# Attention and binary convolutions on one core: the weighted sums laid out as four column tiles of 32 channels over all 128 rows of keys

## The chip, the core and the metric

One NeuronCore of a Trainium2 chip runs the whole kernel. The metric is device time in microseconds (us), the median of the runs. TensorE makes the matrix products, ScalarE the exponentials and some copies, VectorE elementwise work and sums, GpSimd (POOL) and SyncE (SP) issue transfers. Matrix products go to PSUM, eight banks of 512 fp32 columns on each of 128 partitions.

## The reference

The input x has 8 images of 64 channels and 64 x 64 pixels, fp32. Two layers follow each other.

The first is attention among the N = 4096 pixels of one image, with C = 64 channels:

```
q, k, v = wq x + bq, wk x + bk, wv x + bv        # 1x1, per pixel
q, k    = q - mean(q), k - mean(k)               # over pixels
sim     = softmax(q^T k / sqrt(C))               # N x N per image
out     = sim v + (one vector per image from a second softmax)
x       = x + out
```

The second takes the signs of x, applies binarized convolutions of 1x1, 3x3 and 5x5, normalizes and adds the three, and returns the sum times a gate per channel, plus x.

What matters here is the product `sim v`: for each query pixel n the sum over all 4096 key pixels m of exp(score[n, m]) times v[:, m], divided by the sum of the exponentials.

## The kernel before, in words

**Tiling.** Two images form a pair; their 2 x 64 channels fill the 128 partitions, and there are four pairs. Of a pair, 512 query pixels are a block (QB = 512): eight blocks per pair, 32 in all. The keys go in tiles of 128 (NK = 32 steps per block). The very last block is cut into two parts (`PARTS`): 384 queries in 32 steps, and 128 queries in 8 steps of four key tiles each.

**One step.** `scores` (L573) makes four products for key tile j, one for each half h of its 128 keys and each image b: 64 channels are contracted, 64 keys are the stationary columns and 512 queries stream. They lie in the four 64x64 quarters of TensorE's array, and their results fill a PSUM tile of two banks, keys on partitions, one bank per image. ScalarE takes the exponential of both banks at once (L595) into e, 128 keys x 2 images x 512 queries. `weighted` (L598) contracts over the keys: for each image b and key half h it multiplies the values v (64 keys by 64 channels) with e. It too lies in the four 64x64 quarters. The two halves h of the keys[...] each has a bank of its own, acc0 and acc1, which holds the partial sum over its half of all keys. `summed` (L615) adds the e tiles up for the softmax denominator on VectorE, except for four tiles per block that transfers add up in DRAM.

**The end of a block.** `weighted_out` (L627) copies the two banks to SBUF, o0 by ScalarE (L632) and o1 by VectorE (L633); later `added` (L713) adds the two on VectorE (L717) into x2; `finish` (L719) multiplies by the reciprocals and adds the second softmax's vector and x. Then come the signs for the convolutions.

**The order** is written out by hand; nothing reorders it. The loop in `attend` (L1371) issues `scores` of step j, then `weighted` and `summed` of step j-1, and then what `plan` has put down for step j with `put(step, function)`. At step 0 of a block the last weighted group of the block before is issued, its `weighted_out`, and `mix_rows` (L1125): the queries of the next block and the convolutions of the block three back, as products in 64x64 quarters. `mix_rows` uses acc0, acc1, the score banks and two further banks (m); the convolution products that it leaves in acc0 and acc1 are copied out by `hold`, on ScalarE (L939) and VectorE (L937), and after that the next block's weighted sums begin in them. `added` stands at step 13, `finish` at 15. Of the result tiles x2 there are ten buffers, since they are kept until `store` writes the pair's output in the third and fourth block of the next pair. The tiles o0 and o1 share their buffers with the row differences of the convolutions (`rows5`, `rows3`).

TensorE leaves the 64x64 quarters in a few places only: a 128x128 product once per pair (`unary_end`, L461), one 64x128 product (L223), the column sums of the last block (`sums_wide`, L696, 128 rows by 64 columns), and the beginning and the end of the program.

A slow path at the end of the program (from L1484) is entered only where a softmax without its maximum subtracted would have left the range of fp32; it uses the same functions and is not run on these inputs.

Of the kernel before, what the change touches and what calls it, by code (L numbers as in the profile page):

```python
# [18 lines left out]
F32 = mybir.dt.float32  # L19
# [3 lines left out]
ALU = mybir.AluOpType  # L23
# [3 lines left out]
P = 128  # L27
# [4 lines left out]
QB = 512  # L32
NQ = N // QB
NK = N // P
# [13 lines left out]
def conv_seq_kernel(ctx, tc, x, wqv, wk, wv, w1, w3, w5, wtap, gw, out):  # L48
    nc = tc.nc
# [3 lines left out]
    img = [slice(0, C), slice(C, P)]  # L53
# [3 lines left out]
    bp = ctx.enter_context(tc.tile_pool(name="blocks", bufs=10))  # L57
    ep = ctx.enter_context(tc.tile_pool(name="ep", bufs=5))
    fp = ctx.enter_context(tc.tile_pool(name="fp", bufs=1))
# [3 lines left out]
    ps_a = ctx.enter_context(tc.tile_pool(name="ps_a", bufs=1, space=PSUM))  # L63
# [215 lines left out]
    class Pair:  # L279
# [3 lines left out]
        def __init__(self, name, xt):  # L283
            self.name, self.x = name, xt
            self.xs = sm.tile([P, 8], F32, tag="xs", name=f"xs_{name}")
            self.q, self.x2, self.s, self.y1, self.acc, self.o = {}, {}, {}, {}, {}, {}
            self.sides = []
            self.es, self.r, self.joint, self.sc, self.gap, self.t = {}, {}, None, None, None, None

# [308 lines left out]
        def weighted(self, qb, j, e, part=(slice(0, QB), 1)):  # L598
            cols, n = part
            w = cols.stop - cols.start  # L600
            if j == 0:
                self.acc[qb] = acc_banks(f"acc_{self.name}_{qb}_{cols.start}")
            for t in range(n * j, n * j + n):
                at = (t - n * j) * w
                for b in range(2):
                    for h in range(2):
                        nc.tensor.matmul(  # L607
                            self.acc[qb][h][img[b], 0:w],
                            self.v[img[h], t, img[b]],
                            e[img[h], b, at : at + w],  # L610
                            start=(t == 0),
                            stop=(t == NK - 1),
                        )

        def summed(self, qb, j, e, dram=False, begin=nc.vector):  # L615

# [10 lines left out]
        def weighted_out(self, qb, cols=slice(0, QB)):  # L627

            acc, w = self.acc.pop(qb), cols.stop - cols.start
            if cols.start == 0:  # L630
                self.o[qb] = [self.tile(fp, f"o{h}", qb) for h in range(2)]
            nc.scalar.copy(self.o[qb][0][:, cols], acc[0][:, 0:w])  # L632
            nc.vector.tensor_copy(self.o[qb][1][:, cols], acc[1][:, 0:w])  # L633

# [68 lines left out]
        def reciprocals_wide(self, qb, cols):  # L705
            if cols.start == 0:
                self.r[qb] = self.tile(fp, "r", qb)
            for a in range(cols.start, cols.stop, P):
                c = slice(a, min(a + P, cols.stop))
                sums, at = self.sums_p  # L710
                nc.vector.reciprocal(self.r[qb][:, c], sums[:, c.start - at : c.stop - at])

        def added(self, qb, cols=slice(0, QB)):  # L713
            if cols.start == 0:
                self.x2[qb] = self.tile(bp, "x2", qb)
            o = self.o[qb]
            nc.vector.tensor_tensor(self.x2[qb][:, cols], o[0][:, cols], o[1][:, cols], ALU.add)  # L717

        def finish(self, qb, cols=slice(0, QB)):  # L719
            x2 = self.x2[qb][:, cols]  # L720
# [486 lines left out]
    def acc_banks(name):  # L1207
        return [ps_a.tile([P, QB], F32, tag=f"acc{h}", name=f"{name}_{h}") for h in range(2)]

    def misc_banks(name):  # L1210
        return [m_tile(f"{name}_{h}") for h in range(2)]

# [4 lines left out]
    def attend(pairs, early):  # L1217
# [9 lines left out]
        def plan(g):  # L1227


            at = {}  # L1230

            def put(i, f, *a):
                at.setdefault(i, []).append((f, a))

            pr, qb = divmod(g, NQ)
# [34 lines left out]
            if g >= 1:  # L1270
                put(5, p.fold_first, b)
                put(6, p.fold, b)
                put(7, p.fold_last, b)
                put(8, p.spread, b)
                put(9, p.check_block, b, 0)
                put(11, p.check_block, b, 1)
                at0 = 13 if g < n_blocks - 1 else 11
                put(at0, p.added, b)
                put(at0 + 2, p.finish, b)
                put(at0 + (3 if g < n_blocks - 1 else 4), p.signs_wide, b, 2)  # L1280
                put(at0 + (5 if g < n_blocks - 1 else 6), p.signs_wide, b, 1)
                put(at0 + 7, p.signs, b)
# [63 lines left out]
        def plan_last():  # L1346

            at, (first, _) = {}, PARTS
            for i, steps in plan(n_blocks - 1).items():
                at[i * QB // first[0].stop] = steps  # L1350

            def put(i, f, *a):
                at.setdefault(i, []).append((f, a))

            p, b = pairs[-1], NQ - 1
            cols = first[0]
            r1 = cols.stop // HH
            put(NK - 5, lambda: mix(None, rows(n_blocks - 3), one_bank, score_banks))
            put(NK - 2, lambda: mix(None, (p, p.joint_rows(0, 6)), one_bank, score_banks))
            put(NK, p.weighted_out, b, cols)  # L1360
            put(NK + 1, p.added, b, cols)
            put(NK + 1, p.sums_wide, b, first)
            put(NK + 1, p.reciprocals_wide, b, cols)
            put(NK + 2, p.finish, b, cols)
            put(NK + 3, lambda: p.check(p.r[b][:, cols], n_blocks - 1))
            put(NK + 4, p.signs_wide, b, 2, 0, r1)
            put(NK + 5, p.signs_wide, b, 1, 0, r1)
            put(NK + 6, p.signs, b, 0, r1)
            return at
# [28 lines left out]
        r0, r1 = cols.start // HH, ROWS  # L1398
        p.weighted_out(b, cols)
        p.sums_wide(b, part)  # L1400
        p.added(b, cols)
        p.reciprocals_wide(b, cols)
        p.check(p.r[b][:, cols], n_pairs * (NQ + 1), (0,))
        p.finish(b, cols)
# [1 line left out]
            p.signs_wide(b, n, r0, r1, None)  # L1406
            p.copy_signs(b, n, r0, r1, (nc.vector.tensor_copy, nc.gpsimd.tensor_copy))
        p.signs(b, r0, r1, nc.gpsimd.tensor_copy)

        def acc_bank(h):  # L1410
            return lambda name: [ps_a.tile([P, QB], F32, tag=f"acc{h}", name=name)]

        def count(side):
            p.check(p.r[b][:, cols], n_pairs * (NQ + 1), (side,))
# [69 lines left out]
    with tc.If(n_good < P):  # L1484
        neg = fp.tile([P, QB], F32, tag="t5", name="neg")
        nc.vector.memset(neg, 0.0)
        with tc.For_i(0, n_pairs * P, P) as row:
            rows = bass.ds(row, P)
            p = Pair("g", load_x("g", rows))
            for c in range(4):  # L1490
                p.mean_part(c, quarters[c])
            p.mean_sum()
            p.mean_scores()
            p.mean_scores_out()
            p.minus_mean_scores()
            p.value_weights()
            p.shifted_unary()
            for g in range(NQ):
                p.values(g, unary=False)
            for qb in range(NQ):  # L1500
                mix((p, qb), None)
                for h in range(QB // P):
                    part = sm.tile([P, 2, NQ], F32, tag="part", name=f"part_{qb}_{h}")
                    for kb_ in range(NQ):
                        ps = ps_s.tile([P, 2, QB], F32, tag="s", name=f"px_{qb}_{h}_{kb_}")
                        for b in range(2):
                            nc.tensor.matmul(
                                ps[:, b, :],
                                p.q[qb][img[b], bass.ts(h, P)],
                                p.x[img[b], bass.ts(kb_, QB)],  # L1510
                                start=True,
                                stop=True,
                            )
                        nc.vector.tensor_reduce(part[:, :, kb_], ps, AX.X, ALU.max)
                    nm = sm.tile([P, 2], F32, tag="nmx", name=f"nmx_{qb}_{h}")
                    nc.vector.tensor_reduce(nm, part, AX.X, ALU.max, negate=True)
                    pn = m_tile(f"pn_{qb}_{h}")
                    for b in range(2):
                        nc.tensor.matmul(
                            pn[C * b : C * b + 1, 0:P], nm[:, b : b + 1], ident, start=True, stop=True  # L1520
                        )
                        nc.vector.tensor_copy(
                            neg[C * b : C * b + 1, bass.ts(h, P)], pn[C * b : C * b + 1, 0:P]
                        )
                for j in range(NK):
                    e = p.scores(qb, j, neg)
                    p.weighted(qb, j, e)
                    p.summed(qb, j, e)
                p.weighted_out(qb)
                p.sums_wide(qb)  # L1530
                p.reciprocals_wide(qb, slice(0, QB))
                p.added(qb)
                p.finish(qb)
            p.copy_tile()
            for qb in range(NQ):
                for n in (1, 2):
                    p.signs_wide(qb, n)
            for qb in range(NQ):
                p.signs(qb)
                mix(None, (p, p.rows(qb)), acc_banks, score_banks)  # L1540
            p.gate_mean()
            p.gate()
            for qb in range(NQ):
                p.store(qb, rows)
# [57 lines left out]
```

## Time and profile before

| | |
|---|---|
| median of the runs before | 1893.41 us (2 runs, 1893.37 to 1893.46) |
| the profiled execution's span, first to last instruction | 1889.9 us |
| the profiled execution's own time | not given apart; the median lies 3.5 us above the span |
| TensorE busy | 1875.6 us (99%) |
| VectorE busy | 1602.8 us (85%) |
| ScalarE busy | 1269.5 us (67%) |
| GpSimd busy | 131.2 us (7%) |
| granted TensorE clock, mean | 0.999 |

The profile lists instructions in groups: line of the code, engine, operation, output and inputs by name, tile (rows*columns of the array) and shape, count; then the busy time of the group, the mean duration of one in ns, and how long the engine stood idle before them, with what ended that. PE is TensorE; PEld are its weight loads, which have records of their own. A fp32 matmul has two records, as it goes through the array in two passes. Ends of matmuls are modelled, starts are recorded. The chain of waits goes back from the last instruction, at each step to what released it. In the timeline, neighbours of one kind are merged: start, length from the first start to the last end, what, and how many records.

### The profile page before, as it was taken

To read this page: it belongs to the slowest core of one execution; us is meant where nothing else is said; L and a number is where in the kernel's file an instruction comes from. 1 tells how busy PE (TensorE), PEld (TensorE's weight loads), DVE (VectorE), ACT (ScalarE), POOL (GpSimd) and SP (SyncE) were. 2 spreads that over 40 slices of the span, in tenths; PEclk is the share of its full clock that TensorE was granted. 3 is DMA by queue.
4 is the path that set the end of the run, shared out by engine and by line. 5 is a ranking of instruction groups with operands and counts; after the bars stand their busy time and mean duration, and the time that the engine had idled before them with its cause. 6 is when DMAs were issued, how large, how long until landed. Compare 5 with 4: busy or idle time off the path is not lost.

```text
span 1889.9 us, 51407 instructions
## 1 busy us (share of the span) xinstructions
PE 1875.6 (99%) x22016; PEld 800.7 (42%) x22016; DVE 1602.8 (85%) x2526; ACT 1269.5 (67%) x1630; POOL 131.2 (7%) x176
## 2 busy tenths in 40 slices
PE   9999999999999999999999999999999999999997
PEld 4345344443344434443434444434433344444345
DVE  7888888889888888888888888888888888888886
ACT  6666776666666676666666667666666666666664
POOL 0000000000000000000000000000000000000001
PEclk9999999999999999999999999999999999999999
DMA  4334333333333433333333444243333333333311
GB/s 125 65 65 103 78 67 71 67 58 72 68 70 89 117 82 81 65 73 66 58 72 68 97 111 89 58 83 66 72 67 58 71 78 90 86 71 65 82 36 53
DMA packets 73461, 142.50 MB, mean 75 GB/s; under 512 B 10444, under 2 KB 41480, under 8 KB 73096
## 3 DMA queue, kind: packets, MB, share of 16 engines
q0 software_dynamic: 22320, 81.27, 23.3%
q1 hardware_dynamic: 50328, 56.73, 10.3%
q8 instruction: 174, 2.85, 0.6%
q10 hardware_dynamic: 576, 1.13, 0.2%
q14 instruction: 63, 0.52, 0.1%
HBM read 39.27 MB, written 89.78 MB: 68 GB/s over the span
## 4 chain that ended last, share of the span: by engine, by line
PE 98%; DVE 1%; ACT 0%; DMA 0%; issue 0%; ACTq 0%; DVEq 0%
PE ps L582 46%; PE acc L607 46%; PE z L906 2%; PE pv L414 1%; PE z L996 1%; PE pq L563 1%; DMA es<-e 0%; PE z_5e L906 0%; ACT e L595 0%; PE warm L157 0%; DVE es L625 0%; DVE sb L1069 0%; PE pq L535 0%; PE su L696 0%; DVE es_j L1028 0%
## 5 line engine op out<-in xcount | busy, mean ns | idle before, releaser
L595 ACT ACTIVATE e<-ps 128x1024 f32<-128x1024 f32 (+1 forms) x1030 | 1048.4, 1018 | 568.2 <-PE ps L582 553.0
L625 DVE TENSOR_TENSOR es<-es,e 128x1024 f32<-128x1024 f32 (+1 forms) x842 | 1019.7, 1211 | 192.5 <-ACT e L595 178.2
L582 PE MATMUL ps<-q,x 64*64 64x512 f32 (+2 forms) x8448 | 1090.3, 577 | 1.5 <-DVE q L347 0.8
L607 PE MATMUL acc<-e,v 64*64 64x512 f32 (+2 forms) x8432 | 1085.8, 576 | 1.3 <-ACT e L595 1.3
L607 PEld LDWEIGHTS acc<-e,v 64*64 64x64 f32 x8432 | 335.0, 131 | 545.8 <-ACT e L595 314.8
L582 PEld LDWEIGHTS ps<-q,x 64*64 64x64 f32 x8448 | 359.5, 133 | 483.3 <-issue 262.3
L646 POOL DMA_DIRECT2D es<-e x93 | 80.1, 861 | 903.8 <-ACT e L595 598.7
L976 DVE SCALAR_TENSOR_TENSOR sb<-pt,sb 128x256 f32<-128x256 f32 x174 | 65.8, 418 | 0.0
L906 PEld LDWEIGHTS <-wc 64*64 64x64 bf16 x3364 | 58.8, 106 | 1.7 <-issue 0.8
L646 POOL DMA_DIRECT2D es<-es x31 | 26.6, 857 | 438.6 <-DVE es L625 438.6
L623 DVE TENSOR_TENSOR es<-e,e 128x1024 f32<-128x1024 f32 (+1 forms) x31 | 37.7, 1216 | 17.2 <-ACT e L595 17.2
L906 PE MATMUL z<-ec,wc 64*64 64x128 bf16 x1392 | 51.5, 217 | 0.0
L906 PE MATMUL z<-t,wc 64*64 64x128 bf16 x1392 | 51.1, 216 | 0.1
L754 ACT ACTIVATE s<-x,wqv_s 128x512 bf16<-128x512 f32 (+2 forms) x66 | 46.2, 702 | 0.2 <-DVE x L722 0.2
L939 ACT ACTIVATE pt<-z,frac 128x256 f32<-128x256 f32 (+1 forms) x58 | 30.6, 578 | 16.8 <-PE z L906 16.8
L644 POOL DMA_DIRECT2D es<-e x31 | 17.5, 563 | 334.5 <-ACT e L595 323.3
L633 DVE COPY o<-acc 128x512 f32<-128x512 f32 (+2 forms) x33 | 22.3, 675 | 9.4 <-PE acc L607 9.3
L950 DVE TENSOR_TENSOR pt<-pt 128x384 f32<-128x384 f32 x58 | 29.6, 552 | 0.0
L414 PEld LDWEIGHTS pv<-wx,x 64*64 64x64 f32 x992 | 21.5, 134 | 16.1 <-issue 8.6
L661 DVE TENSOR_TENSOR e_parts<-e_parts 128x512 f32<-128x512 f32 x31 | 21.3, 686 | 6.1 <-DMA e_parts<-es 6.0
L722 DVE SCALAR_TENSOR_TENSOR x<-x,ou,x 128x512 f32<-128x512 f32 (+2 forms) x33 | 24.3, 736 | 1.2
L422 ACT COPY v<-pv 128x512 f32<-128x512 f32 x31 | 18.2, 587 | 8.4 <-PE pv L414 8.4
(201 smaller groups left out, 893.9 us busy)
## 6 DMA issues: line engine op xcount, KB each, us to landing
es<-e POOLq DMA_DIRECT2D x124, 512.0 KB, 5.1
es<-es POOLq DMA_DIRECT2D x31, 512.0 KB, 5.3
e_parts<-es SPq DMA_DIRECT2D x124, 128.0 KB, 3.0
r<-rc SPq DMA_DIRECT2D x62, 128.0 KB, 2.8
out<-sb SPq DMA_DIRECT2D x27, 256.0 KB, 2.9
x<-in_x SPq DMA_DIRECT2D x24, 256.0 KB, 4.3
ec<-t SPq DMA_DIRECT2D x29, 99.0 KB, 4.5
xc<-in_x SPq DMA_DIRECT2D x30, 72.0 KB
```

Of the source, the lines that this page charges most:

```text
L414: nc.tensor.matmul(pv[img[h], b, i * w : (i + 1) * w], self.x[img[b], bass.ds((4 * g + i) * P + h * H, H)], self.wx[img[b], 0:w], start=Tr ...
L582: nc.tensor.matmul(ps[img[h], b, i * w : (i + 1) * w], self.x[img[b], bass.ds((n * j + i) * P + h * H, H)], self.q[qb][img[b], cols], star ...
L595: nc.scalar.activation(e, ps[:, :, 0 : n * w], AF.Exp, scale=1.0 / 8.0)
L607: nc.tensor.matmul(self.acc[qb][h][img[b], 0:w], self.v[img[h], t, img[b]], e[img[h], b, at : at + w], start=(t == 0), stop=(t == NK - 1),)
L623: begin.tensor_tensor(self.es[qb], self.first, e, ALU.add)
L625: nc.vector.tensor_tensor(self.es[qb], self.es[qb], e, ALU.add)
L646: nc.gpsimd.dma_start(out=out, in_=e, accum_op=ALU.add)
L754: nc.scalar.activation(sy[n][0][:, rows, pad : pad + HH], self.x2[qb][:, r0 * HH : r1 * HH].rearrange("p (h w) -> p h w", w=HH), AF.Sign, ...
L906: nc.tensor.matmul(z[img[b], :].rearrange("p (q w) -> p q w", w=HH), wc[k][img[h], n, c * C : c * C + C], src[:, first : first + step + 1 ...
L939: nc.scalar.activation(out, z, AF.Identity, scale=frac[:, by : by + 1])
L950: nc.vector.tensor_tensor(self.pairs[:, :, :, r, :], t[:, 0:3, 0], t[:, 0:3, 1], op)
L976: nc.vector.scalar_tensor_tensor(out, x, by, out, ALU.mult, ALU.add, **gap)
```

## The change

`weighted` no longer cuts the array into 64x64 quarters. Each key tile is contracted over all its 128 keys at once, and the 128 output channels of the two images are cut into four column tiles of 32: g = 0, 1 for the first image and 2, 3 for the second. There are still four products per key tile, each with 512 streaming columns. The two key halves no longer need two partial sums, so one bank, acc0, holds the result; `weighted_out` copies it by ScalarE straight into x2, and the copy by VectorE and `added` are gone. x2 is therefore taken at step 0 of the following block instead of step 13. `acc_bank`, which stood inside `attend`, moves out unchanged. `mix_rows` still uses acc0 and acc1. `scores` and all else stay.

```diff
@@ weighted
             if j == 0:
-                self.acc[qb] = acc_banks(f"acc_{self.name}_{qb}_{cols.start}")
+                self.acc[qb] = acc_bank(0)(f"acc_{self.name}_{qb}_{cols.start}")[0]
             for t in range(n * j, n * j + n):
                 at = (t - n * j) * w
-                for b in range(2):
-                    for h in range(2):
-                        nc.tensor.matmul(
-                            self.acc[qb][h][img[b], 0:w],
-                            self.v[img[h], t, img[b]],
-                            e[img[h], b, at : at + w],
-                            start=(t == 0),
-                            stop=(t == NK - 1),
-                        )
+                for g in range(4):
+                    nc.tensor.matmul(
+                        self.acc[qb][32 * g : 32 * g + 32, 0:w],
+                        self.v[:, t, 32 * g : 32 * g + 32],
+                        e[:, g // 2, at : at + w],
+                        start=(t == 0),
+                        stop=(t == NK - 1),
+                    )
@@ weighted_out
             if cols.start == 0:
-                self.o[qb] = [self.tile(fp, f"o{h}", qb) for h in range(2)]
-            nc.scalar.copy(self.o[qb][0][:, cols], acc[0][:, 0:w])
-            nc.vector.tensor_copy(self.o[qb][1][:, cols], acc[1][:, 0:w])
+                self.x2[qb] = self.tile(bp, "x2", qb)
+            nc.scalar.copy(self.x2[qb][:, cols], acc[:, 0:w])
...
-        def added(self, qb, cols=slice(0, QB)):
-            if cols.start == 0:
-                self.x2[qb] = self.tile(bp, "x2", qb)
-            o = self.o[qb]
-            nc.vector.tensor_tensor(self.x2[qb][:, cols], o[0][:, cols], o[1][:, cols], ALU.add)
...
+    def acc_bank(h):
+        return lambda name: [ps_a.tile([P, QB], F32, tag=f"acc{h}", name=name)]
...
@@ plan, plan_last, the end of attend and the slow path: the calls of added
-                put(at0, p.added, b)
...
-            put(NK + 1, p.added, b, cols)
...
-        p.added(b, cols)
...
-                p.added(qb)
```

More of the change, by code (lines that the diff above doesn't have):

```diff
@@ L285, in __init__ @@
             self.xs = sm.tile([P, 8], F32, tag="xs", name=f"xs_{name}")
-            self.q, self.x2, self.s, self.y1, self.acc, self.o = {}, {}, {}, {}, {}, {}
+            self.q, self.x2, self.s, self.y1, self.acc = {}, {}, {}, {}, {}
             self.sides = []
@@ L1408, in attend @@
         p.signs(b, r0, r1, nc.gpsimd.tensor_copy)
-        def acc_bank(h):
-            return lambda name: [ps_a.tile([P, QB], F32, tag=f"acc{h}", name=name)]
         def count(side):
```

## The prediction

> **What bounds the kernel now.** I read the page's first part, then the chain that ended last, then the costliest groups.
>
> ```profile
> PE 1875.6 (99%) x22016; PEld 800.7 (42%) x22016; DVE 1602.8 (85%) x2526; ACT 1269.5 (67%) x1630; POOL 131.2 (7%) x176
> ...
> PE 98%; DVE 1%; ACT 0%; DMA 0%; issue 0%; ACTq 0%; DVEq 0%
> ...
> L582 PE MATMUL ps<-q,x 64*64 64x512 f32 (+2 forms) x8448 | 1090.3, 577 | 1.5 <-DVE q L347 0.8
> L607 PE MATMUL acc<-e,v 64*64 64x512 f32 (+2 forms) x8432 | 1085.8, 576 | 1.3 <-ACT e L595 1.3
> ```
>
> TensorE is the bound: busy 99%, 98% of the chain, and its two big groups, the scores (L582) and the weighted sums (L607, the line that changes), waited 1.5 and 1.3 us in all. VectorE and ScalarE follow: the list of waits has ScalarE's exponentials waiting for the scores for 553.0 us. So whatever leaves VectorE or ScalarE is worth almost nothing, and whatever a step adds on TensorE is added to the time. A busy TensorE could still hide slack, so I looked at the pitch in the timeline of TensorE, in the middle of the run (start, length of the merged piece, what):
>
> ```profile
> 900.93 1.06 PE L607 MATMUL acc<-e,v 64*64 64x512 f32 x8
> 901.79 1.06 PE L582 MATMUL ps<-q,x 64*64 64x512 f32 x8
> 902.64 1.06 PE L607 MATMUL acc<-e,v 64*64 64x512 f32 x8
> ```
>
> Each group of four fp32 matmuls (eight records: every fp32 matmul is two passes) starts 0.86 us after the one before; from 900.93 to 906.08 there are six, so 0.858 each. The four 64x64 tiles run at once, so a group is two passes of 512 columns, 0.429 us each, 0.838 ns per column. The 1.06 us is longer than the pitch: groups overlap at their ends. There is no slack in the pitch to win.
>
> Now the places where TensorE changes the layout of its tiles. First a 128*128 product (L461) between two 64*64 groups; then a 128*64 product (L696), the only kind with two column tiles over all 128 rows:
>
> ```profile
> 1404.88 1.06 PE L607 MATMUL acc<-e,v 64*64 64x512 f32 x8
> 1405.87 0.49 PE L461 MATMUL po<-vu,ones 128*128 128x130 f32 x2
> 1406.29 1.09 PE L582 MATMUL ps<-q,x 64*64 64x512 f32 x8
> 1407.20 0.61 PE L607 MATMUL acc<-e,v 64*64 64x512 f32 x4
> ```
> ```profile
> 1855.82 0.72 PE L607 MATMUL acc<-e,v 64*64 64x128 f32 x20
> 1856.48 0.87 PE L696 MATMUL su<-es,ones 128*64 128x384 f32 x4
> 1857.27 0.56 PE L582 MATMUL ps<-q,x 64*64 64x128 f32 x12
> ```
>
> The group that a switch ends lasts 1405.87-1404.88 = 0.99 us instead of 0.86: **0.13 us at the exit**. The same exits at 479.38 and 81.39 us last 1.00 and 0.97. The group that begins after a switch lasts 1407.20-1406.29 = 0.91: **0.05 us at the entry**. L461 itself takes 0.42 against 2 x 130 x 0.838 = 0.22 of streaming, 0.20 more; less an exit of 0.10 that is an entry of 0.10, twice that of the 64-column groups: the exposed part is the first weight load, by columns. L696 shows the same: 0.79 against 2 x 384 x 0.838 = 0.64, so 0.15 more (0.05 and 0.10), and its four records fit in two passes, so two column tiles over all 128 rows did run at once.
>
> **What the Trainium skill says.** "TensorEngine Tiling (Array Packing)", Tiling Modes: changing the tiling mode, not only the tile, drains the engine. The trace agrees, 0.10 to 0.14 us at each exit. "TensorE: Matmul & The Clock Gate", LDWEIGHTS: a load takes its columns divided by 1.2, in ns, whatever the rows; for 64 columns 53 ns, the 0.05 us seen. The same page, Part 3: column tiles of 32 overlap (three of them gave 2.38x); the trace shows only two of 64. "Perfetto Trace Analysis", Tensor Engine Instruction: the end of a matmul in the profile is an estimate; so I use differences of starts only.
>
> **The change, part by part.**
>
> 1. *The products.* Before: four of 64 rows and 64 columns of weights; after: four of 128 rows and 32. Same count, same 512 moving columns, four at once: 0.858 us of streaming either way, gain nil. The trace doesn't show four column tiles over all rows. Bounds: 0 (as the two in L696) to a halved rate, +0.858 us per group. I take 0, for L696's reason.
>
> 2. *The layout switches.* The loop issues the scores of step j, then the weighted sums of step j-1, in turn. Scores stay 64*64, so each weighted group now has a switch before and one after. Groups: 31 blocks of 32 steps, the last one's 32 of 384 columns and 8 of 128 (four tiles of keys each): 992 + 32 + 8 = 1032. (Check: 992 x 8 + 32 x 8 + 8 x 32 = 8448 records, the 8432 and 16 that the trace has.) Each step pays: exit of the scores 0.11, entry of the weighted group by 32 columns 0.025 (half of 0.05, an estimate from the 64- and 128-column entries), its exit 0.11, entry of the scores 0.05. Sum **0.295 us**, and 1032 x 0.295 = **304 us**. For the exit I take 0.11, the 81.39 case, where all the groups before it ran at the regular pitch; in the two others the mix ahead had spread the tiles' starts. Bounds per step: 0.23 (exits 0.09, what is left when the 0.02 by which the first and the last of four tiles start apart (7 ns from one to the next in the records of the group at 1406.29) is hidden, no entry for the weights of 32 columns) to 0.405 (exits 0.14, both entries 0.05, and 0.025 for a second pass's load that is not hidden): 237 to 418 us.
>
> 3. *Second copy and addition gone* (L633: 22.3 us in 33 records; L717: 31 x 0.686 + two short ones, about 22 us). Both are on VectorE, which TensorE doesn't wait for; priced at nothing. The last pair, at 1869.6 to 1870.3, is beside the convolutions that TensorE runs without a gap from 1870.71 to 1875.9: also nothing, at most 0.3 us.
>
> 4. *ScalarE's copy stays* (579 ns, L632), now into the result. Its new wait is for a buffer of x2, taken 13 steps sooner; behind it on ScalarE stand the exponentials. There are ten buffers; in the closest case the earlier user is read last by a store at step 15 of the third block of a pair, and the buffer is wanted again at step 0 of the fourth, 17 steps later: nothing. If that cover were gone it would stall ScalarE, which has 620 us idle.
>
> 5. *One bank instead of two.* After the mix of a block, the first weighted group waits for the bank's last reader, the copy of convolution products by ScalarE (17.7 us of weight-load wait in 29 blocks before), now of one bank, not both. The load was let go about 0.07 us ahead of its matmuls' turn (1404.81 and 1404.88); after the change that turn comes later by the exit of the scores. Nothing; without that cover 29 x 0.1 = 3 us.
>
> 6. *Other engines.* The step grows from 1.717 to 2.01 us; the exponential (1.018 us) and the sum on VectorE (1.211 us) fit with more room. They just wait longer.
>
> Sum against the profiled execution: span 1889.9 + 304 = 2193.9; the median of the runs, 1893.41, is 3.5 us above that span, which I keep: **2197 us**, 16% slower. Own range 1893.4 + 237 to 1893.4 + 418: 2130 to 2311.
>
> **The rivals.**
>
> *A: four column tiles over all rows do not stream at full rate.* Each row of the array would feed four different column tiles with fp32, where the scores feed two; nothing in the trace runs so. If they go two by two, each weighted group has 0.858 us more: 1032 x 0.858 = 885, time 2197 + 885 = 3082. Against it: L696's two tiles at full rate, and the skill's three. Chance 0.11.
>
> *B, the other side: the switch is hidden.* Place: the 2064 borders between L582 and L607. Mechanism: the layouts share column bounds and the weights of the next one are loaded behind the running group, so the border costs what it does now. Price 0, time 1893, no change. It decides if a border costs under 1893.4 x 0.02 / 2064 = 18 ns. Against it: the smallest that any of the switches above shows is 100 to 150 ns with its entry, and those between 64*64 and 128*64 are no cheaper than those to 128*128. Chance 0.05.
>
> *C: the tiles don't overlap at all,* so the change doesn't do what it says: three more streams of 0.858 us per group, 1032 x 2.574 = 2656, time about 4850. Against it: L696. Chance 0.03.
>
> **How the numbers follow.** My forecast has 0.81; A 0.11, B 0.05, C 0.03. The range 2130 to 2310 is the forecast's own; the others leave out 0.19. Slower by over 2% (about what a measurement of this kernel can tell from no change): forecast, A and C, 0.95. Within 2%: B but for 0.01, so 0.04; faster 0.01.
>
> **What would show it.** In the timeline after: scores and weighted groups alternate at about 1.02 and 1.00 us instead of 0.86, each with eight records; weight loads of a group start only when the group before has ended, instead of inside it; the idle time of TensorE appears as short gaps or longer first passes. VectorE's busy time falls by about 44 us and its share to about 71%, with no effect on the end. Wrong if the weighted group's pitch is 1.8 us or more (A or C), if the pitch stays 0.86 (B), or if ScalarE's copy becomes what TensorE waits for at the start of each block.

## The result and the profile after

The changed kernel takes **2190.82 us** (2 runs, 2190.74 to 2190.90) against 1893.41 us before: ratio 1.157, 95% interval 1.1537 to 1.1604. It is 16% slower. Its profiled execution spans 2189.0 us, 299.1 us more than before.

The page of the kernel after, its first part, its chain and the two big groups:

```profile
PE 2176.3 (99%) x22016; PEld 486.1 (22%) x22016; DVE 1584.7 (72%) x2460; ACT 1274.9 (58%) x1630; POOL 131.1 (6%) x176
...
PE 99%; DVE 0%; DMA 0%; ACT 0%; SPq 0%; issue 0%; DVEq 0%
...
L582 PE MATMUL ps<-q,x 64*64 64x512 f32 (+2 forms) x8448 | 1115.2, 600 | 1.1 <-DVE q L347 0.8
L606 PE MATMUL acc<-e,v 128*32 128x512 f32 (+2 forms) x8432 | 1090.9, 591 | 0.1
```

TensorE is busy 99% as before, 301 us longer, with the same number of instructions and the same granted clock, 0.999. These lines alone would hide the cause: the busy time of the two groups, 1090.3 and 1085.8 us before, has grown by 24.9 and 5.1 us only. It was that large before because neighbouring groups overlapped in it, and now they hardly do. The mean durations say nearly nothing either (577 to 600 and 576 to 591 ns). What tells it is the pitch, the time from the start of one group to the start of the next. The timeline of TensorE after, in the middle of the run:

```profile
1045.24 1.07 PE L606 MATMUL acc<-e,v 128*32 128x512 f32 x8
1046.23 1.09 PE L582 MATMUL ps<-q,x 64*64 64x512 f32 x8
1047.26 1.07 PE L606 MATMUL acc<-e,v 128*32 128x512 f32 x8
1048.25 1.09 PE L582 MATMUL ps<-q,x 64*64 64x512 f32 x8
```

A weighted group lasts 0.99 us until the next group starts, a score group 1.02 to 1.03, where both had 0.86. The lengths of the pieces (1.07 and 1.09) are about those of before (1.06): a piece ends in a modelled tail of some 0.07 us into the next group, where it was 0.2.

The place of the 128*128 product, the model for the estimate, looks after the change like this:

```profile
1628.33 1.07 PE L606 MATMUL acc<-e,v 128*32 128x512 f32 x8
1629.33 0.49 PE L461 MATMUL po<-vu,ones 128*128 128x130 f32 x2
1629.75 1.09 PE L582 MATMUL ps<-q,x 64*64 64x512 f32 x8
1630.77 1.06 PE L606 MATMUL acc<-e,v 128*32 128x512 f32 x8
```

That place is now no exception: the weighted group ahead of it lasts 1.00 as everywhere, L461 still 0.42, and the scores behind it 1.02, since they too are left by a switch.

The weight loads show a part of the reason. First the timeline of the loads before, then that after:

```profile
902.33 0.15 PEld L607 LDWEIGHTS acc<-e,v 64*64 64x64 f32 x4 [0.37 <-ACT e L595]
902.65 0.17 PEld L607 LDWEIGHTS acc<-e,v 64*64 64x64 f32 x4 [0.16 <-issue]
```
```profile
1046.23 0.21 PEld L582 LDWEIGHTS ps<-q,x 64*64 64x64 f32 x8 [0.84 <-PE ps L582]
1047.25 0.16 PEld L606 LDWEIGHTS acc<-e,v 128*32 128x32 f32 x8 [0.81 <-ACT e L595]
```

Before, the weighted group that began at 902.64 had its first four loads at 902.33, inside the scores. After, all eight loads start with the group, at 1047.25, and none stands ahead of it. The reason given for the wait (ScalarE's e) is only the semaphore that came last; ScalarE was done early (its exponential ran from 1045.38 for 1.02 us), and in the list of waits it now waits longer for TensorE itself:

```profile
ACT e L595 <- PE ps L582: 844.2, 1007, 2.9
```

That was 553.0 us before.

The unmerged starts, those of the single passes, of the step at 1046.23 take the 0.299 us apart. The last of the scores' second passes starts at 1046.735 and the first weighted pass at 1047.255: 0.520, of which 0.429 is streaming. In the other 0.09 nothing new starts; this is called the drain here. The other border has it too (1047.729 to 1048.250). First and second pass of one tile start 0.481 apart in the scores and 0.454 in the weighted group, instead of 0.429: 0.052 for a first load of 64 columns and 0.025 for one of 32. And the four tiles of a group start 7 ns apart, 0.020 from first to last. In the kernel before, each tile of a group follows its own predecessor after 0.429, so this costs nothing; now the next group starts only behind the last tile. Sum: 2 x 0.091 + 0.052 + 0.025 + 2 x 0.020 = 0.299.

### The profile page after: what moved, and what is told of

Read it like the earlier page. It is cut to its first block, busy times and chain, and to the rows that moved or that the text cites. A ratio compares the mean times of both kernels' runs of the same rounds, so it can differ in the third digit from the quotient of the medians.

```text
span 2189.0 us, 51341 instructions
## 1 busy us (share of the span) xinstructions
PE 2176.3 (99%) x22016; PEld 486.1 (22%) x22016; DVE 1584.7 (72%) x2460; ACT 1274.9 (58%) x1630; POOL 131.1 (6%) x176
## 4 chain that ended last, share of the span: by engine, by line
PE 99%; DVE 0%; DMA 0%; ACT 0%; SPq 0%; issue 0%; DVEq 0%
PE ps L582 47%; PE acc L606 47%; PE z L898 2%; PE pv L414 1%; PE pq L563 1%; PE z L988 1%; DMA x<-in_x 0%; PE z_5e L898 0%; DVE sb L1061 0%; PE su L694 0%; PE po L461 0%; DVE sb L1020 0%; DVE es_j L1061 0%; DVE es L624 0%; PE pq L535 0%
## 5 line engine op out<-in xcount | busy, mean ns | idle before, releaser
L595 ACT ACTIVATE e<-ps 128x1024 f32<-128x1024 f32 (+1 forms) x1030 | 1047.5, 1017 | 848.7 <-PE ps L582 844.2
L582 PE MATMUL ps<-q,x 64*64 64x512 f32 (+2 forms) x8448 | 1115.2, 600 | 1.1 <-DVE q L347 0.8
L606 PE MATMUL acc<-e,v 128*32 128x512 f32 (+2 forms) x8432 | 1090.9, 591 | 0.1
L582 PEld LDWEIGHTS ps<-q,x 64*64 64x64 f32 x8448 | 225.7, 131 | 794.4 <-PE ps L582 740.1
L606 PEld LDWEIGHTS acc<-e,v 128*32 128x32 f32 x8432 | 167.5, 108 | 823.6 <-ACT e L595 582.5
L570 DVE TENSOR_SCALAR q<-pq,mx 128x224 f32<-128x224 f32 x30 | 13.5, 451 | 37.9 <-PE pq L563 37.9
L422 ACT COPY v<-pv 128x512 f32<-128x512 f32 x31 | 18.1, 585 | 17.7 <-PE pv L414 17.7
L929 DVE TENSOR_SCALAR pt<-z,frac 128x256 f32<-128x256 f32 x29 | 14.0, 484 | 18.5 <-PE z L898 18.5
```

The costliest lines, as they stand in the source:

```text
L582: nc.tensor.matmul(ps[img[h], b, i * w : (i + 1) * w], self.x[img[b], bass.ds((n * j + i) * P + h * H, H)], self.q[qb][img[b], cols], star ...
L595: nc.scalar.activation(e, ps[:, :, 0 : n * w], AF.Exp, scale=1.0 / 8.0)
L606: nc.tensor.matmul(self.acc[qb][32 * g : 32 * g + 32, 0:w], self.v[:, t, 32 * g : 32 * g + 32], e[:, g // 2, at : at + w], start=(t == 0), ...
```

## The experiments

The theory: each step pays for leaving and entering a layout twice, and nothing else of the change matters. The rivals: the 128*32 products themselves are slow; the single bank or the direct copy makes TensorE wait; VectorE's lost work is worth something.

### The layout alone

```diff
 # from the kernel before; both copies and added stay
-                for b in range(2):
-                    for h in range(2):
...
+                for g in range(4):
+                    nc.tensor.matmul(
+                        self.acc[qb][t % 2][32 * g : 32 * g + 32, 0:w],
+                        self.v[:, t, 32 * g : 32 * g + 32],
+                        e[:, g // 2, at : at + w],
+                        start=(t < 2),
+                        stop=(t >= NK - 2),
+                    )
```

> The new layout alone: the weighted sums on four 128*32 column tiles, but even key tiles go to acc0 and odd ones to acc1, both banks are copied out by ScalarE and VectorE, and added stays. My theory (two layout switches per step, 0.299 us as the trace after shows it) expects the time after, 2191 us within 5, since VectorE's work and the second bank are worth nothing. The rival that the single bank or the copy straight into x2 makes TensorE wait at the start of a block expects it to be clearly below 2191, by 31 times what such a wait costs. If the copy and the addition that were removed had been worth something, it is above 2191.

Measured: 2191.01 us (4 runs, 2190.59 to 2191.12), ratio 1.1578 (1.1559 to 1.1598). The first line of its page:

```profile
PE 2176.3 (99%) x22016; PEld 486.2 (22%) x22016; DVE 1623.8 (74%) x2526; ACT 1272.7 (58%) x1630; POOL 131.1 (6%) x176
```

VectorE works 39.1 us more than in the changed kernel and TensorE is busy for the same 2176.3 us. So the layout makes the whole difference; the bank, the copy and the addition together make none that is seen.

### Half as many switches, and the order's control

```diff
...
-                new = (p, (qb, j, e), part)
-                if pending is not None:
-                    pending[0].weighted(*pending[1], pending[2])
...
-                for f, a in at.pop(i, ()):
-                    f(*a)
-                pending = new
+                waiting.append((p, (qb, j, e), part))
+                if i % 2 == 0:
+                    continue
+                due = waiting[:-2]
+                for d in due:
+                    d[0].weighted(*d[1], d[2])
+                for d in due:
+                    begin = nc.gpsimd if d[2] == PARTS[1] else nc.vector
+                    d[0].summed(*d[1], g < n_blocks - 1, begin)
+                waiting = waiting[-2:]
+                for f, a in [*at.pop(i - 1, ()), *at.pop(i, ())]:
+                    f(*a)
...
```

Made once to the changed kernel:

> The changed kernel with the loop issuing two score groups and then two weighted groups, so that 516 pairs of switches are left of 1032. My theory expects half of the loss: 1893 + 516 x 0.299 = 2047 us less a few, 2035 to 2050, with the second group of each two starting 0.86 us after the first. The rival that the loss sits in the 128*32 products themselves (slower streaming of four column tiles over all rows) expects the time to stay at 2191, and the rival that waits on ScalarE grow with this order expects more.

and once to the kernel before:

> The control for the order: the kernel before, with the same loop of two score groups and two weighted groups, all in 64*64 tiles. Every theory of the layout expects 1893 us within 10. If it is well below or above, the order itself is worth something, and the paired 128*32 kernel is to be compared with this one.

Measured: 2064.90 us (2064.88 to 2065.48), ratio 1.0913 (1.0894 to 1.0931), for the first, and 1927.24 us (1926.64 to 1927.72), ratio 1.0184 (1.0167 to 1.0201), for the control. Both miss what was expected: the order is not free. The timeline of the control, and then that of the 128*32 kernel:

```profile
1002.11 1.90 PE L582 MATMUL ps<-q,x 64*64 64x512 f32 x16
1003.82 1.90 PE L607 MATMUL acc<-e,v 64*64 64x512 f32 x16
1005.54 1.90 PE L582 MATMUL ps<-q,x 64*64 64x512 f32 x16
```
```profile
1000.68 1.92 PE L606 MATMUL acc<-e,v 128*32 128x512 f32 x16
1002.54 1.95 PE L582 MATMUL ps<-q,x 64*64 64x512 f32 x16
1004.41 1.92 PE L606 MATMUL acc<-e,v 128*32 128x512 f32 x16
```

In the middle of a block the control runs at the pitch of before, 1.71 to 1.72 for two groups, so its 35 us are lost elsewhere. The starts in its trace show where. The two score groups behind the mix of a block take 2.47 us instead of 1.72, some 16 us in all; of the 20.2 us for which its scores stood idle (1.5 before), 12.2 lie there, until the copy of convolution products on VectorE (L944) is done. And once in nearly every block, in 29 of them, the scores behind a weighted pair start 0.2 to 1.7 us late and then take 0.1 us more: 14 us. In 27 of these places ScalarE's exponential had waited for VectorE, which cost 0.7 us in all before:

```profile
ACT e L595 <- DVE rec L671: 82.4, 27, 4.3
```

The new loop does two steps' other work in one place, which is likely why; no run takes that apart.

Two 128*32 groups need 1.86 and two score groups with them 1.87 to 1.88, together 0.30 more than the control. That is one pair of switches for two steps, and a second 128*32 group behind a first costs just its streaming: 1.86 is 0.86 and one 1.00. Against its control the kernel loses 137.7 us, 0.267 for each of 516 pairs, where the pitch says 0.30, 154 us. Of the 16 us between, 14 are the late scores: the trace of the 128*32 kernel has the long groups behind the mix too (2.58 instead of 1.88), but no late ones. Halving the switches has taken 42% of the loss away from the changed kernel in time, and half of it from the pitch. Slow 128*32 products would have kept it all.

### The price of two switches alone

```diff
 # from the kernel before, at the head of weighted, ahead of its products
+            if j > 0:
+                nc.tensor.matmul(
+                    self.acc[qb][0][0:32, 0:1], wu[:, 0:32], e[:, 0, 0:1], start=False, stop=False
+                )
```

> The price of two switches alone: the kernel before, its products all in 64*64 tiles, with one added product per step from the second of a block on: 128 rows, 32 columns of zero weights and one moving column, added into the first 32 partitions of acc0 ahead of the weighted group (999 of them). My theory expects each to cost what the weighted groups pay now, 0.299 us, and up to 0.1 more for its own two short passes: 1893 + 999 x 0.30 to 0.40 = 2190 to 2290 us. The rival that the loss sits in the weighted products themselves, not in the switches, expects at most 999 x 0.1, so below 1993.

The control has the same line with 64 rows and 64 columns, `acc[qb][0][img[0], 0:1], wu[img[0], img[0]], e[img[0], 0, 0:1]`:

> The control for the added product: the kernel before, with the same added product of one moving column per step, but on 64 rows and 64 columns of zero weights, so that the layout never changes. My theory expects only the issue of two short passes, no drain: 0 to 0.08 us each, 1893 to 1975 us. The rival that any product added between the groups breaks the overlap, whatever its layout, expects as much as with the 128*32 one, 2190 us or more.

Measured: 2197.33 us (2196.88 to 2198.47), ratio 1.1613 (1.1594 to 1.1632), for the 128*32 one: 305.2 us over the 1892.13 us of before beside it, 0.306 for each of 999. The control took 2002.86 us (2002.15 to 2004.90), ratio 1.0584 (1.0566 to 1.0602): 0.110 each, more than the 0 to 0.08 expected and far less than the rival's. The timeline of TensorE with the 128*32 product:

```profile
1003.18 0.22 PE L604 MATMUL acc<-e,wu 128*32 128x1 f32 x2
1003.34 1.09 PE L611 MATMUL acc<-e,v 64*64 64x512 f32 x8
1004.25 1.04 PE L582 MATMUL ps<-q,x 64*64 64x512 f32 x8
1005.22 0.22 PE L604 MATMUL acc<-e,wu 128*32 128x1 f32 x2
```

The scores (1004.25 to 1005.22) last 0.97, which is 0.11 of drain and exposed starts; the one-column product 0.15 to 0.16, with its own two short passes and a drain; the weighted group, of 64*64 tiles as before, 0.91, which is 0.05 of entry. A product that adds only zeros costs as much as the whole change, with all useful products in their old form. The two prices are not made of the same parts, so that they are so close is in part chance: this one has the product's own passes in it, and lacks the starts of four tiles. The weight loads of the control:

```profile
1000.59 0.13 PEld L604 LDWEIGHTS acc<-e,wu 64*64 64x64 f32 x1 [0.76 <-ACT e L595]
1000.60 0.15 PEld L611 LDWEIGHTS acc<-e,v 64*64 64x64 f32 x3
1000.64 0.13 PEld L604 LDWEIGHTS acc<-e,wu 64*64 64x64 f32 x1
1000.65 0.23 PEld L611 LDWEIGHTS acc<-e,v 64*64 64x64 f32 x5
```

The added product's quarter has a load at 1000.59, its second at 1000.64, and only then one for its useful pass. In the next step, which is a plain one, the loads of this quarter start at 1002.473, 1002.530 and 1002.588 in the unmerged records: two times 0.057 to 0.058, with no long pass of the quarter between them to hide behind, make 0.115, about the price. If that is so, four such products on four quarters cost what one does.

### Four added products instead of one

```diff
+            for g in range(4 * (j > 0)):
+                c = slice(32 * g, 32 * g + 32)
+                nc.tensor.matmul(self.acc[qb][0][c, 0:1], wu[:, c], e[:, g // 2, 0:1], start=False, stop=False)
```

> As the kernel with one added 128*32 product of zeros per step (2197 us), but with four, one on each column tile, next to each other. If the price is that of leaving and entering a layout, it is paid once for all four: 0.305 us as for one, and up to 0.03 for four starts instead of one, 2197 to 2230 us. If each added product has a price of its own, the time rises by as much again for each of the three more, towards 3100.

and with four of 64 rows and 64 columns, one on each quarter:

> As the kernel with one added 64*64 product of zeros per step (2003 us, 0.110 us each), but with four, one on each quarter of the array. If the 0.110 is two weight loads of 64 columns[...] that no long pass of the same quarter hides, the four quarters pay it side by side: 2003 to 2030 us. If every product added costs 0.110, it is 1893 + 999 x 0.44 = 2333 us. Either way the difference to the four 128*32 products is what two changes of layout cost.

Measured: 2217.68 us (2217.51 to 2217.85), ratio 1.1719 (1.1699 to 1.1738), and 2003.43 us (2002.76 to 2003.97), ratio 1.0587 (1.0569 to 1.0604). Neither price is one per product. Four 128*32 products cost 20.4 us more than one, 0.020 a step, three starts of 7 ns; four 64*64 ones cost what one did. The timelines, first without and then with the change of layout:

```profile
1001.90 1.04 PE L582 MATMUL ps<-q,x 64*64 64x512 f32 x8
1002.76 0.24 PE L605 MATMUL acc<-e,wu 64*64 64x1 f32 x8
1002.85 1.07 PE L612 MATMUL acc<-e,v 64*64 64x512 f32 x8
```
```profile
1003.14 1.04 PE L582 MATMUL ps<-q,x 64*64 64x512 f32 x8
1004.11 0.24 PE L605 MATMUL acc<-e,wu 128*32 128x1 f32 x8
1004.28 0.66 PE L610 MATMUL acc<-e,v 64*64 64x512 f32 x4
```

The scores last 0.86 without a switch behind them and 0.97 with one. Between these two kernels, with the same number and length of products, lie 214 us, 0.214 for two switches. Two drains of 0.09 are 0.18; the rest has the exposed starts in it, and the difference between weights of 32 and of 64 columns, so that it is no clean price of the switch.

### Rows alone, columns alone

```diff
 # from the changed kernel: two column tiles of 64, all 128 rows
+                for b in range(2):
+                    nc.tensor.matmul(
+                        self.acc[qb][img[b], 0:w],
+                        self.v[:, t, img[b]],
+                        e[:, b, at : at + w],
...
 # from the kernel before: column tiles of 32, 64 rows, eight tiles
+                for g in range(4):
+                    c = slice(32 * g, 32 * g + 32)
+                    for h in range(2):
+                        nc.tensor.matmul(
+                            self.acc[qb][h][c, 0:w],
+                            self.v[img[h], t, c],
+                            e[img[h], g // 2, at : at + w],
...
```

> The changed kernel with two column tiles of 64 channels over all 128 rows instead of four of 32, one per image. Against the scores' layout only the rows change. My theory: the same number of switches, streaming the same; the entry pays 64 columns of weights (0.05) instead of 32 (0.025), 1032 x 0.025 = 26 us more, and two starts instead of four (7 ns each, 14 ns less per pass order) take back up to 14 us: 2191 to 2217, likeliest 2203. The rival that the drain is owed to the narrow column tiles expects about 1893.

> The kernel before with each weighted product cut in two column tiles of 32: eight tiles of 64 rows and 32 columns, two banks, both copies and added kept. Against the scores' layout only the columns change. If a change of the columns alone drains as the change of both does, the loss is about 1032 x 0.3, and four more starts of 7 ns per group add up to 1032 x 0.03: 2190 to 2230 us. If only a change of the rows drains, it is 1893 to 1930 us. My theory takes any change as a switch and expects the first.

Measured: 2204.79 us (2204.43 to 2205.05), ratio 1.1647 (1.1627 to 1.1666), and 2222.54 us (2221.46 to 2224.14), ratio 1.1744 (1.1724 to 1.1763). The timelines, 128*64 and then 64*32:

```profile
1000.77 1.08 PE L606 MATMUL acc<-e,v 128*64 128x512 f32 x4
1001.78 1.09 PE L582 MATMUL ps<-q,x 64*64 64x512 f32 x8
```
```profile
1000.78 1.09 PE L608 MATMUL acc<-e,v 64*32 64x512 f32 x16
1001.80 1.09 PE L582 MATMUL ps<-q,x 64*64 64x512 f32 x8
```

Both weighted groups last 1.01 to 1.02 us. A change of the rows alone drains, and so does one of the columns alone: from the last start of a group to the first start behind it there are 0.519 to 0.523 us at each border of these steps, 0.09 more than the streaming. The smaller terms are right too: 128*64 is 14.0 us above the changed kernel, 0.0136 a step, and 0.027 for 64 columns of weights instead of 32, less two starts of 7 ns, is 0.013. All three forms, with two, four and eight tiles, stream at the rate of the four quarters; for 128*32 the paired kernel shows it without a switch, for the two others it follows from these sums.

## Why the prediction was right, and by how much it was off

*What bounds the kernel.* Right: TensorE is 99% busy in both, and its pitch carried the time. With the layout alone changed, 39 us more on VectorE made no difference.

*1, the products.* Right: four column tiles over all rows stream at full rate. Two neighbouring 128*32 groups in the paired kernel show it at 1.86. Rivals A and C, which needed the opposite, are out.

*2, the switches.* Right in mechanism and nearly in size. Per plain step 0.295 was predicted and 0.299 is the pitch's excess in the trace (scores 0.16, weighted 0.14). Each term holds: exits of 0.11 are 0.09 of drain and 0.02 of exposed starts; entries 0.052 and 0.025.

The exit of 0.11 looks like a lucky pick. It came from a product of another layout, 64*128, and there is a fourth exit in the trace before, which the prediction left out and which takes 0.27:

```profile
77.22 1.20 PE L607 MATMUL acc<-e,v 64*64 64x512 f32 x8
78.35 0.49 PE L461 MATMUL po<-vu,ones 128*128 128x130 f32 x2
```

But the reason given for the pick, that elsewhere the tiles' starts were spread, holds in the unmerged records. Counted from the last start of the group instead of the first, all four exits take the same: 77.828 to 78.347, 479.856 to 480.375, 1405.348 to 1405.867 and 81.842 to 82.361 are 0.519 each, with the 0.09 of drain that the kernel after has.

Over the whole span the excess is 299.1 / 1032 = 0.290, so 9.5 us less than 1032 plain steps would pay. The plain groups, 918 of each kind in the trace after, agree within 2 ns. The scores behind value products (31) and behind the mix (28) are entered without a switch and rose by 0.06 and 0.11 us only, instead of 0.16: 4.4 us of the 9.5. About as much are single waits of the kernel before, whose longest group lasted 1.87 us, that the slower one hardly has. So a term that was 0.004 low and a count of steps that took every step as plain partly offset each other; that is luck, if small. The sum was 4.9 us high on the span. The 3.5 us added for what lies around the span were 1.7 too many: median and span of before were evidently of different executions, for wherever the record has both of one execution they lie 1.7 to 1.9 apart. Together this is the 6.6 us between 2197.4 and 2190.8.

Rival B, the hidden switch, is out: the added products of zeros priced two switches at about 0.2, where 0.036 would have decided for B.

*3, copy and addition gone.* Right as priced, at nothing. The forecast for the busy time was 44 us less; it fell by 18.1. The durations of VectorE's instructions do add up to 43.6 us less (1734.7 before, 1691.1 after); but the page counts overlapping records once, and in the looser timeline neighbours overlap less, by 25.5 us. The step of this side forecast that failed was to subtract a sum of durations from a busy time.

*4 and 5, ScalarE's copy and the single bank.* Right: two banks and the late addition gave the same time within 0.2 us.

*6, others.* Right: ScalarE waited for scores for 844.2 us instead of 553.0.

## What to carry to other kernels

Where TensorE streams without a gap, as here, count the changes of tile layout in the inner loop before counting anything that they save elsewhere: here each pair cost 0.3 us beside 1.72 us of products. A layout that is as good for the products as another is only worth taking for all products of the loop, or in long runs; a single tiny product in another layout cost as much here as four large ones. Read the pitch, from start to start, since the busy time of a group hardly moved.

## What the runs showed of the hardware

- Each change of layout seen here drains TensorE, for 0.09 us: of rows alone (64*64 to 128*64), of columns alone (to 64*32, and to 64*128 in the kernel before), or of both (to 128*32 and 128*128). Four products between two changes cost what one did, but for their starts of 7 ns.
- Behind a change the first weight load is exposed: first and second pass start 0.454 us apart with 32 columns of weights and 0.481 with 64, instead of 0.429.
- A short product is not free even in the same layout: one moving column on one quarter cost 0.110 us, and on all four quarters at once no more. The loads of that quarter, 64 columns each and 0.057 us apart, account for it.
- Fp32 products on two (128*64), four (128*32) and eight (64*32) tiles stream equally fast, 0.429 us for a pass of 512 columns, also where every row of the array feeds four column tiles.
